# Layers 0 and 1 of a four-layer graph network: one-value-a-token rows spread through DRAM, attention applied to x before W, seven lanes for five

## Chip, cores, metric

One core of one Trainium2 chip. The metric is the device time of one execution in microseconds, median of several runs. In the profile's lines PE is TensorE, PEld its weight loads, DVE VectorE, ACT ScalarE, POOL GpSimd and SPq the queue of SyncE, which issues the DMA transfers; L550 is line 550 of that kernel; a record is one TensorE instruction in the trace. Ratios are the mean time of one kernel's fast runs over the mean of the other's fast runs in the same rounds, so they are not quite the ratios of the medians quoted beside them. Kernels of one batch of experiments ran on one chip beside the kernel before; kernels of different batches are compared by these ratios.

## The reference

x is 64 graphs x 256 nodes x 128 features, fp32; adj is one 256 x 256 matrix of zeros and ones. Four layers, each `x = layernorm(x + layer(x))`. Only the first two are changed:

```python
# layer 0
h = x @ others_weight
u1, u2 = h @ a1, h @ a2                      # one value a token
e = leaky(u1[:, idx1] + u2[:, idx2], 0.1)    # idx1, idx2: index pairs of a 256 x 256 grid
out = softmax(where(adj > 0, e, NEG_BIG), axis=1) @ h + x @ self_weight
# layer 1
h = x @ W
e = leaky((h @ a_src)[:, :, None] + (h @ a_dst)[:, None, :], 0.2)   # again one value a token
out = elu(softmax(where(adj + I == 0, -1e9, e), axis=-1) @ h)
# layer 2: five steps of a gated recurrent unit over adj;  layer 3: Chebyshev sums
```

Both attention layers need rows in which every partition holds one value for each token.

## The kernel before

The work is cut into 32 units of two graphs (512 tokens). A plan, computed in Python when the kernel is built, simulates the engines with one assumed duration for every instruction, takes the ready instruction of the oldest unit each time, and issues all instructions in that static order. Five units ("lanes") are in flight. On the chip each engine then runs its own list in order: an instruction that waits holds everything behind it on its engine.

```python
LATENCY = {"pe": 220, "dve": 150, "act": 150, "pool": 200, "sp": 3000}   # ns, from issue's end to use

def seen_at(self, t, by):            # when task `by` may count on task t
    return t.end if t.eng != by.eng else t.off + self.OWN[t.eng]
...
t.end = t.off + self.LATENCY[e] + t.wait

# layer 0, per unit (T = 512 tokens)                                       ... cut
xT = feature_major(u, L)                                    # 4 transposes
matmul(ps_c, wc_b, xT)                                      # L408: the row, by a broadcast matrix
matmul(ps_d[:, b:b+1], xb[:, b, k:N:2], wu[:, k:k+1])       # L412: x4, one column each
matmul(hx[b][:, c], xb[:, b, c*P:(c+1)*P], wx0)             # L423: x [W, self], 256 columns, x4
...                                                         # scores, exp, sums
matmul(hxv(b)[:, ic, 1], p[...], h[...])                    # L458: attention times h, x8
# layer 1
xT = feature_major(u, L)                                    # 4 transposes
matmul(ps_h[b][...], xb[:, b, c*P:(c+1)*P], wx1)            # L473: x4
matmul(ps_e, ws_b, xT)                                      # L477: the row
activation(e[:, g], ps_e[:, b*N:(b+1)*N], Prelu, bias=h[:, g, D:D+1])   # L486
...
matmul(ov()[:, ic], p[...], h[...])                         # L504: attention times h, x8
```

The softmax here doesn't subtract the row's maximum and nothing guards it: scores larger than these inputs give would overflow.

## Time and profile before

| | before |
|---|---|
| median, range | 1639.08 us, 1638.92 to 1639.25 (4 runs) |
| span, TensorE busy | 1637.2 us, 1615.9 us |
| mean granted TensorE clock | 0.999 |
| sum of TensorE's waits that the trace names | 13.7 us |

The prediction shows the engine shares, the chain and the waits. Two more lines of the page are needed for comparison: the granted clock in 40 slices (tenths of full speed), and the DMA packets by size.

```profile
PEclk9999999999999999999999999999999999999999
DMA packets 36731, 19.42 MB, mean 12 GB/s; under 512 B 2465, under 2 KB 36513, under 8 KB 36641
```

TensorE keeps 0.9 or more of its clock in every slice (0.999 on average), and 2465 of 36731 packets are under 512 bytes.

### The profile page before, as it was taken

The page shows a single profiled execution, that of the slowest core. Times are in us where ns is not written, and L with a number is a line of the kernel's source. Part 1 is how long each engine was busy: PE and PEld are TensorE (multiplying, and loading weights), DVE is VectorE, ACT ScalarE, POOL GpSimd, SP SyncE. Part 2 cuts the span into 40 slices and gives each one's busy share as a digit, 9 for nine tenths or more (in the row PEclk, how much of TensorE's full clock was granted, in tenths as well). Part 3 has the DMA queues.
Part 4 walks back from the last instruction along what each step waited for, and adds up shares of the span by engine and source line. Part 5 has one row for each costly group of instructions (what it writes and reads, how often), then busy time and mean ns, then how long its engine had stood idle before and what let it go on. Part 6 is the DMA issues. An engine that isn't in the chain of part 4 may idle for free.

```text
span 1637.2 us, 18751 instructions
## 1 busy us (share of the span) xinstructions
PE 1615.9 (99%) x6999; PEld 1095.2 (67%) x6999; DVE 950.4 (58%) x2214; ACT 820.2 (50%) x1602; POOL 145.7 (9%) x134
## 2 busy tenths in 40 slices
PE   8899999999999999999999999999999999999998
PEld 7556667666667666676666666667666667765566
DVE  6844556655556655466555665555656556763544
ACT  4644445544554545454455544545545544654542
POOL 0100001100001100011000110001101011100001
PEclk9999999999999999999999999999999999999999
DMA  9000000000000000000000000000000000000000
GB/s 241 1 0 7 7 7 8 7 1 7 7 7 7 7 1 7 7 8 7 1 7 7 7 7 1 7 7 7 7 1 7 7 7 7 7 1 0 1 7 26
DMA packets 36731, 19.42 MB, mean 12 GB/s; under 512 B 2465, under 2 KB 36513, under 8 KB 36641
## 3 DMA queue, kind: packets, MB, share of 16 engines
q1 hardware_dynamic: 36640, 18.23, 4.2%
q8 instruction: 55, 0.90, 0.2%
q14 instruction: 36, 0.29, 0.1%
HBM read 9.84 MB, written 8.39 MB: 11 GB/s over the span
## 4 chain that ended last, share of the span: by engine, by line
PE 94%; DVE 3%; ACT 1%; POOL 0%; issue 0%; DMA 0%; POOLq 0%; DVEq 0%; ACTq 0%
PE ps L543 41%; PE ps L527 20%; PE ps L597 7%; PE ps L570 4%; PE ps L604 3%; PE ps L423 3%; PE ps L375 3%; PE ps L504 3%; PE ps L458 3%; PE ps L408 2%; PE ps L473 2%; PE ps L477 2%; PE ps L412 1%; DVE x L395 1%; DVE st L386 0%; POOL rstd L391 0%
## 5 line engine op out<-in xcount | busy, mean ns | idle before, releaser
L543 PE MATMUL ps<-m,gT 128*128 128x512 f32 x960 | 463.7, 595 | 1.0 <-ACT e L549 0.6
L391 POOL TENSOR_TENSOR rstd<-ve,nhalf 128x4 f32<-128x4 f32 x128 | 145.0, 1134 | 1485.7 <-DVE ve L388 1459.0
L543 PEld LDWEIGHTS ps<-m,gT 128*128 128x128 f32 x960 | 173.1, 190 | 135.3 <-issue 116.2
L527 PE MATMUL ps<-adjT,ht 128*128 128x256 f32 x1024 | 253.6, 381 | 0.5 <-ACT ht L574 0.5
L551 DVE SCALAR_TENSOR_TENSOR e<-e,xT 128x512 f32<-128x512 f32 x160 | 110.3, 690 | 205.0 <-ACT e L549 204.5
L527 PEld LDWEIGHTS ps<-adjT,ht 128*128 128x128 f32 x1024 | 188.1, 190 | 54.9 <-issue 27.4
L562 DVE TENSOR_TENSOR p<-p,xT 128x512 f32<-128x512 f32 x160 | 110.3, 689 | 175.8 <-ACT p L556 175.3
L558 ACT ACTIVATE e<-ps,bias 128x512 f32<-128x512 f32 x160 | 109.9, 687 | 146.6 <-PE ps L543 146.6
L539 ACT COPY m<-ps 128x512 f32<-128x512 f32 x160 | 93.7, 585 | 174.4 <-PE ps L527 168.8
L543 PE MATMUL ps<-xT,gT 128*128 128x512 f32 x320 | 164.2, 595 | 0.5 <-ACT xT L377 0.5
L543 PE MATMUL ps<-e,u5T 128*128 128x512 f32 x320 | 163.0, 597 | 0.9 <-DVE e L551 0.8
L549 ACT ACTIVATE e<-ps,bias 128x512 f32<-128x512 f32 x160 | 109.9, 687 | 106.7 <-PE ps L543 106.0
L527 PE MATMUL ps<-adjT,x 128*128 128x256 f32 x512 | 143.6, 380 | 0.0
L570 PEld LDWEIGHTS ps<-ident,xT 128*128 128x128 f32 x640 | 83.7, 141 | 76.6 <-issue 53.4
L556 ACT ACTIVATE p<-ps,bias 128x512 f32<-128x512 f32 x160 | 109.9, 687 | 35.2 <-PE ps L543 34.8
L574 ACT COPY ht<-ps 128x512 f32<-128x512 f32 x128 | 74.6, 585 | 97.6 <-PE ps L570 96.8
L563 DVE SCALAR_TENSOR_TENSOR p<-e,p 128x512 f32<-128x512 f32 x160 | 110.2, 689 | 21.8 <-ACT e L558 18.7
L570 PE MATMUL ps<-ident,xT 128*128 128x128 f32 x640 | 118.7, 274 | 0.6 <-DVE xT L565 0.4
L395 DVE TENSOR_SCALAR x<-ps,st,rstd 128x128 f32<-128x128 f32 x256 | 93.4, 404 | 41.6 <-POOL rstd L391 41.0
L375 PE MATMUL ps<-ident,x 128*128 128x128 f32 x512 | 112.5, 276 | 1.6 <-DVE x L395 1.1
L377 ACT COPY xT<-ps 128x512 f32<-128x512 f32 x128 | 74.6, 585 | 78.6 <-PE ps L375 78.1
L565 DVE SCALAR_TENSOR_TENSOR xT<-p,xT 128x512 f32<-128x512 f32 x160 | 110.0, 687 | 2.9
(107 smaller groups left out, 2046.4 us busy)
## 6 DMA issues: line engine op xcount, KB each, us to landing
x<-in_x_dram SPq DMA_DIRECT2D x32, 256.0 KB, 5.5
out_dram<-x SPq DMA_DIRECT2D x32, 256.0 KB, 2.3
wk<-in_L_gnn_weight_dram SPq DMA_DIRECT2D x1, 448.0 KB, 5.2
gate<-in_L_gnn_w_w_dram SPq DMA_DIRECT2D x3, 128.0 KB, 3.4
adj_t<-in_adj_dram SPq DMA_DIRECT2D x1, 256.0 KB, 2.6
u<-in_L_gnn_u_w_dram SPq DMA_DIRECT2D x2, 64.0 KB, 3.0
wo<-L_gnn_others_weight_dram SPq DMA_DIRECT2D x1, 64.0 KB, 2.3
wself<-n_L_gnn_self_weight_dram SPq DMA_DIRECT2D x1, 64.0 KB, 2.8
```

Source lines behind the costliest of these rows:

```text
L375: add(PE, 110, lambda g=g: nc.tensor.transpose(ps.ap[:, g * P : (g + 1) * P], X[u].ap[:, g // NC, g % NC, :], ident.ap), (X[u], ident), (ps,))
L391: add(POOL, 1050, lambda: nc.gpsimd.tensor_tensor(rstd.ap, ve.ap, nhalf.ap, op=ALU.pow), (ve, nhalf), (rstd,))
L527: add(PE, mm_ns(N), lambda b=b, mc=mc: nc.tensor.matmul(ps.ap[:, b * N : (b + 1) * N], (src.ap if len(src.ap.shape) == 4 else src.ap.rearr ...
L543: add(PE, mm_ns(T), lambda: nc.tensor.matmul(ps.ap, w(), rhs.ap, start=start, stop=stop, skip_group_check=True), (c, rhs), (ps,))
L549: add(ACT, 600, lambda ps_g=ps_g: nc.scalar.activation(r.ap, ps_g.ap, AF.Tanh, bias=bias2.ap[:, 1:2], scale=0.5), (ps_g, bias2), (r,))
L551: add(DVE, 600, lambda h=h: nc.vector.scalar_tensor_tensor(r.ap, r.ap, 1.0, h.ap, op0=ALU.add, op1=ALU.mult), (r, h), (r,))
L556: add(ACT, 600, lambda ps_v=ps_v: nc.scalar.activation(v.ap, ps_v.ap, AF.Tanh, bias=bias2.ap[:, 2:3]), (ps_v, bias2), (v,))
L562: add(DVE, 600, lambda h=h: nc.vector.tensor_sub(v.ap, v.ap, h.ap), (v, h), (v,))
L563: add(DVE, 600, lambda: nc.vector.scalar_tensor_tensor(v.ap, z.ap, 1.0, v.ap, op0=ALU.add, op1=ALU.mult), (v, z), (v,))
L565: add(DVE, 600, lambda h=h, new=new: nc.vector.scalar_tensor_tensor(new.ap, v.ap, 0.5, h.ap, op0=ALU.mult, op1=ALU.add), (v, h), (new,))
L570: add(PE, 110, lambda g=g, h=h, ps_t=ps_t: nc.tensor.transpose(ps_t.ap[:, g * P : (g + 1) * P], h.ap[:, g * P : (g + 1) * P], ident.ap), ( ...
L597: add(PE, mm_ns(N), lambda k=k, src=src, c=c, b=b: nc.tensor.matmul(view(c)[:, :, b, :], bn(src.ap)[:, b, c * P : (c + 1) * P], w3.ap[:, k ...
```

## The change

Intent: take work off TensorE, which is the bound. Attention is applied to x (layer 1), which makes the result feature-major without transposes; rows and pair sums come from extra columns of other products, are stored to DRAM and loaded back with a partition broadcast. Two lanes more are to cover the longer way. The first three units (`DIRECT = 3`) make their rows with broadcast transposes on TensorE instead.

```diff
-LANES = 5
-LEAD = 20
+LANES = 7
+LEAD = 10
+DIRECT = 3
+        c["cu"] = cell(f"cu_{k}", [P, 3, G])
+        c["esd"] = cell(f"esd_{k}", [P, G, 2])
+    def to_row(row, src, view, n):
+        add("sp", 450, lambda: nc.sync.dma_start(row.ap[:, 0 : P * n].rearrange("o (p n) -> (o p) n", p=P), view()), (src,), (row,))
+    def from_row(t, row):
+        add("sp", 450, lambda: nc.sync.dma_start(t.ap, row.ap.rearrange("o n -> (o n)").partition_broadcast(P)), (row,), (t,),
+            wait=2500)
+    def on_all(u, t, row, src, view):
+        if u >= DIRECT:
+            to_row(row, src, view, G)
+            from_row(t, row)
+            return t, lambda: t.ap.rearrange("q (p b c) -> q b c p", b=UB, c=NC)
+        ...                                   # else: 4 transposes into PSUM
 layer 0:
+        row, rv = on_all(u, lc, L["row"], cu, lambda: cu.ap[:, 2])
+            to_row(L["rowu"], cu, lambda: cu.ap[:, 0:2].rearrange("p k g -> p (k g)"), 2 * G)
+            ...                               # two loads of u4 from rowu
+            add(DVE, 100, lambda: nc.vector.tensor_add(d.ap, u4.ap[:, 0:3:2], u4.ap[:, 12:15:2]), (u4,), (d,))
+            add(DVE, 120, ... tensor_mul(esd.ap[:, b * NC : (b + 1) * NC, :], yv()[:, :, D : D + 2], ...), (y, rstd), (esd,))
 layer 1:
-        xT = feature_major(u, L)
-        ...                                   # L473, L477 and the copies of h
+        es, ev = on_all(u, L["m"], L["row"], esd, lambda: esd.ap[:, :, 0])
-            add(ACT, 400, ... activation(e, ps_e, Prelu, bias=h.ap[:, g, D : D + 1]) ...)
+            add(ACT, 400, ... activation(e, ev()[:, b], Prelu, bias=esd.ap[:, g, 1:2]) ...)
+        ...                                   # x p: 8 records of 256 columns; then W
```

(x tiles become a ring of 14 and are loaded as lanes free up; the products of weights at the start are composed anew and centred. Both are cut here.)

More of the change, by code (lines that the diff above doesn't have):

```diff
@@ L190 @@
     PE, DVE, ACT, POOL = "pe", "dve", "act", "pool"
+    C0 = D + 5
     const = ctx.enter_context(tc.tile_pool(name="const", bufs=1))
     psum = ctx.enter_context(tc.tile_pool(name="psum", bufs=1, space=bass.MemoryType.PSUM))
+    dram = ctx.enter_context(tc.tile_pool(name="dram", bufs=1, space=bass.MemoryType.DRAM))
     def sb(name, shape):
@@ L217 @@
     out_u = out.rearrange("(u b) (c p) d -> u p b c d", b=UB, p=P)
-    X = {}
+    xs, X = [cell(f"x{k}", [P, UB, NC, D]) for k in range(2 * LANES)], {}
     def load_x(u):
-        X[u] = load(f"x{u}", x_u[u], [P, UB, NC, D], 1000)
-    adj_t = load("adj_t", adj.rearrange("(c p) j -> p c j", p=P), [P, NC, N])
+        X[u] = c = xs[u % len(xs)]
+        add("sp", 1000, lambda: nc.sync.dma_start(c.ap, x_u[u]), (), (c,))
+    w1 = load("w1", W, [D, D])
+    asd = cell("asd", [D, 2])
+    for k, a in enumerate((a_src, a_dst)):
+        add("sp", 450, lambda k=k, a=a: nc.sync.dma_start(asd.ap[:, k : k + 1], a), (), (asd,))
     wo = load("wo", others_weight, [D, D])
@@ L227 @@
     wself = load("wself", self_weight, [D, D])
+    adj_t = load("adj_t", adj.rearrange("(c p) j -> p c j", p=P), [P, NC, N])
     load_x(1)
-    w1 = load("w1", W, [D, D])
-    asd = cell("asd", [D, 2])
-    for k, a in enumerate((a_src, a_dst)):
-        add("sp", 450, lambda k=k, a=a: nc.sync.dma_start(asd.ap[:, k : k + 1], a), (), (asd,))
     load_x(2)
@@ L243 @@
     wk = load("wk", weight_1, [D, D, 7], 1500)
-    for u in range(4, NU):
+    for u in range(4, LANES):
         load_x(u)
@@ L290 @@
     add(DVE, 420, lambda: nc.vector.tensor_scalar(mask1.ap, mask1.ap, 0.0, None, op0=ALU.is_gt), (mask1,), (mask1,))
-    def projected(name, w, vecs):
-        wT = transposed(name + "T", [(w, w.ap)])
-        ps, t = bank(), cell(name, [P, 2])
-        add(PE, 150, lambda: nc.tensor.matmul(ps.ap[:, 0:2], wT.ap[:, 0], vecs.ap, start=True, stop=True),
-            (wT, vecs), (ps,))
-        add(DVE, 150, lambda: nc.vector.tensor_copy(t.ap, ps.ap[:, 0:2]), (ps,), (t,))
-        return t
-    wu = projected("wu", wo, att)
@@ L301 @@
-    wc = cell("wc", [P, 1])
-    add(DVE, 150, lambda: nc.vector.tensor_add(wc.ap, wu.ap[:, 0:1], wu.ap[:, 1:2]), (wu,), (wc,))
-    wc_b = cell("wc_b", [P, P])
-    add(DVE, 230, lambda: nc.vector.tensor_copy(wc_b.ap, wc.ap.to_broadcast([P, P])), (wc,), (wc_b,))
-    wx0 = cell("wx0", [P, 2, D])
-    add(DVE, 150, lambda: nc.vector.tensor_copy(wx0.ap[:, 0], wo.ap), (wo,), (wx0,))
-    add(DVE, 250, lambda: nc.vector.tensor_add(wx0.ap[:, 1], wself.ap, ident.ap), (wself, ident), (wx0,))
-    wsd = projected("wsd", w1, asd)
@@ L311 @@
-    ws_b = cell("ws_b", [P, P])
-    add(DVE, 230, lambda: nc.vector.tensor_copy(ws_b.ap, wsd.ap[:, 0:1].to_broadcast([P, P])), (wsd,), (ws_b,))
-    wx1 = cell("wx1", [P, D + 1])
-    add(DVE, 150, lambda: nc.vector.tensor_copy(wx1.ap[:, 0:D], w1.ap), (w1,), (wx1,))
-    add(DVE, 150, lambda: nc.vector.tensor_copy(wx1.ap[:, D : D + 1], wsd.ap[:, 1:2]), (wsd,), (wx1,))
+    centre = cell("centre", [P, P])
+    add(DVE, 150, lambda: nc.vector.tensor_scalar_add(centre.ap, ident.ap, -1.0 / D), (ident,), (centre,))
@@ new lines, in product @@
+    def product(ps, at, n, lhs, lhs_ap, rhs, rhs_ap):
+        add(PE, mm_ns(n), lambda: nc.tensor.matmul(ps.ap[:, at : at + n], lhs_ap(), rhs_ap(), start=True, stop=True,
+                                                   skip_group_check=True), (lhs, rhs), (ps,))
+    wx1 = cell("wx1", [P, D + 1])
+    w1cT = cell("w1cT", [P, D])
+    ps_w1, ps_w1T = bank(), bank()
+    product(ps_w1T, 0, D, w1, lambda: w1.ap, centre, lambda: centre.ap)
+    add(DVE, 230, lambda: nc.vector.tensor_copy(w1cT.ap, ps_w1T.ap[:, 0:D]), (ps_w1T,), (w1cT,))
@@ new lines @@
+    product(ps_w1, 0, D, centre, lambda: centre.ap, w1, lambda: w1.ap)
+    add(DVE, 230, lambda: nc.vector.tensor_copy(wx1.ap[:, 0:D], ps_w1.ap[:, 0:D]), (ps_w1,), (wx1,))
+    add(DVE, 60, lambda: nc.vector.memset(wx1.ap[:, D : D + 1], 1.0 / D), (), (wx1,))
+    right0 = cell("right0", [P, C0])
+    ps_r = bank()
+    add(DVE, 150, lambda: nc.vector.tensor_copy(right0.ap[:, 0:D], centre.ap), (centre,), (right0,))
+    product(ps_r, 0, 2, w1cT, lambda: w1cT.ap, asd, lambda: asd.ap)
+    add(DVE, 100, lambda: nc.vector.tensor_copy(right0.ap[:, D : D + 2], ps_r.ap[:, 0:2]), (ps_r,), (right0,))
@@ new lines @@
+    add(DVE, 100, lambda: nc.vector.tensor_copy(right0.ap[:, D + 2 : D + 4], att.ap), (att,), (right0,))
+    add(DVE, 100, lambda: nc.vector.tensor_add(right0.ap[:, D + 4 : D + 5], att.ap[:, 0:1], att.ap[:, 1:2]),
+        (att,), (right0,))
+    woT = transposed("woT", [(wo, wo.ap)])
+    add(DVE, 250, lambda: nc.vector.tensor_add(wself.ap, wself.ap, ident.ap), (wself, ident), (wself,))
+    wselfT = transposed("wselfT", [(wself, wself.ap)])
+    wx0, ws0 = cell("wx0", [P, C0]), cell("ws0", [P, D + 2])
@@ L318 @@
+    for t, wT, n in ((wx0, woT, C0), (ws0, wselfT, D + 2)):
+        ps = bank()
+        product(ps, 0, n, wT, lambda wT=wT: wT.ap[:, 0], right0, lambda n=n: right0.ap[:, 0:n])
+        add(DVE, 230, lambda t=t, n=n, ps=ps: nc.vector.tensor_copy(t.ap, ps.ap[:, 0:n]), (ps,), (t,))
     gs = [cell(f"gs{k}", [D, D]) for k in range(3)]
@@ L354, in lane_cells @@
             c[name] = Cell(c[at].ap.rearrange("p g n -> p (g n)")[:, half * T : (half + 1) * T])
-        c["h0"] = cell(f"h0_{k}", [P, G, D])
-        c["h1"] = cell(f"h1_{k}", [P, G, D + 2])
+        c["h0"] = cell(f"h0_{k}", [P, G, C0])
         c |= {name: cell(f"{name}_{k}", [P, G]) for name in ("nm", "s", "rs", "rstd", "ve")}
@@ L359, in lane_cells @@
         c["st"] = cell(f"st_{k}", [P, UB, 6])
-        add(DVE, 60, lambda: nc.vector.memset(c["h1"].ap[:, :, D + 1 : D + 2], 1.0), (), (c["h1"],))
+        c["u"] = cell(f"u_{k}", [P, 15])
+        c["cu"] = cell(f"cu_{k}", [P, 3, G])
+        c["esd"] = cell(f"esd_{k}", [P, G, 2])
+        for name, n in (("row", T), ("rowu", 2 * T + 2)):
+            c[name] = Cell(dram.tile([1, n], F32, tag=f"{name}_{k}", name=f"{name}_{k}"))
         return c
@@ L378, in feature_major, with layernorm @@
         return L[name]
-    def layernorm(u, L, pairs, swap=False):
+    def to_row(row, src, view, n):
[8 more added lines that the diff above has]
+            return t, lambda: t.ap.rearrange("q (p b c) -> q b c p", b=UB, c=NC)
+        ps = bank()
+        for g in range(G):
+            add(PE, 110, lambda g=g: nc.tensor.transpose(
+                ps.ap[:, g * P : (g + 1) * P], view()[:, g : g + 1].to_broadcast([P, P]), ident.ap), (src, ident), (ps,))
+        return ps, lambda: ps.ap.rearrange("q (b c p) -> q b c p", b=UB, c=NC)
+    def layernorm(u, L, pairs, swap=False, centred=False):
         st, ve, rstd = L["st"], L["ve"], L["rstd"]
@@ L394, in layernorm @@
                 b, ch = (j, k) if swap else (k, j)
+                if centred:
+                    add(DVE, 260, lambda k=k, j=j, b=b, ch=ch, view=view: nc.vector.tensor_scalar(
+                        X[u].ap[:, b, ch, :], view()[:, j, :], rstd.ap[:, 2 * k + j : 2 * k + j + 1], 1.0,
+                        op0=ALU.mult, op1=ALU.add), (c, rstd), (X[u],))
+                    continue
                 add(DVE, 260, lambda k=k, j=j, b=b, ch=ch, view=view: nc.vector.tensor_scalar(
@@ L406, in layer0 @@
         xb = bn(xT.ap)
-        ps_c, ps_d = bank(), bank()
-        tail = [add(PE, mm_ns(T), lambda: nc.tensor.matmul(ps_c.ap, wc_b.ap, xT.ap, start=True, stop=True),
-                    (xT, wc_b), (ps_c,))]
+        lc, d, e, p, h, u4, cu = L["m"], L["d"], L["e"], L["p"], L["h0"], L["u"], L["cu"]
+        nm, s, rs = L["nm"], L["s"], L["rs"]
         for b in range(UB):
-            for k in range(2):
-                tail.append(add(PE, 240, lambda b=b, k=k: nc.tensor.matmul(
-                    ps_d.ap[:, b : b + 1], xb[:, b, k : N : 2], wu.ap[:, k : k + 1], start=(k == 0), stop=(k == 1)),
-                    (xT, wu), (ps_d,)))
@@ L416, in layer0 @@
-        hx = [bank() for _ in range(UB)]
-        def hxv(b):
-            return hx[b].ap.rearrange("p (c k d) -> p c k d", c=NC, k=2)
-        for b in range(UB):
-            for c in range(NC):
-                add(PE, mm_ns(N), lambda b=b, c=c: nc.tensor.matmul(
-                    hx[b].ap[:, c * N : (c + 1) * N], xb[:, b, c * P : (c + 1) * P],
-                    wx0.ap.rearrange("p k d -> p (k d)"), start=(c == 0), stop=True, skip_group_check=True),
-                    (xT, wx0), (hx[b],), tail)
@@ L427, in layer0 @@
-        lc, d, nd, e, p = L["m"], L["d"], L["nd"], L["e"], L["p"]
-        nm, s, rs, h = L["nm"], L["s"], L["rs"], L["h0"]
-        add(ACT, 600, lambda: nc.scalar.activation(lc.ap, ps_c.ap, AF.Prelu, alpha=0.1), (ps_c,), (lc,))
-        add(ACT, 160, lambda: nc.scalar.activation(d.ap, ps_d.ap[:, 0:UB], AF.Prelu, alpha=0.1), (ps_d,), (d,))
-        ev = e.ap.rearrange("p (b c) n -> p b c n", b=UB)
-        add(DVE, 600, lambda: nc.vector.tensor_add(
-            ev[:, :, :, 0:P], lc.ap.rearrange("p (b i c) -> p b c i", b=UB, c=NC),
-            neg0.ap[:, :, 0:P].rearrange("p (o c) n -> p o c n", o=1).to_broadcast([P, UB, NC, P])), (lc, neg0), (e,))
+            hx = bank()
@@ new lines, in hv @@
+            def hv(hx=hx):
+                return hx.ap[:, 0 : NC * C0].rearrange("p (c k) -> p c k", c=NC)
+            for c in range(NC):
+                add(PE, mm_ns(C0), lambda b=b, c=c, hv=hv: nc.tensor.matmul(
+                    hv()[:, c, :], xb[:, b, c * P : (c + 1) * P], wx0.ap, start=(c == 0), stop=True,
+                    skip_group_check=True), (xT, wx0), (hx,))
+            add(ACT, 400, lambda b=b, hv=hv: nc.scalar.copy(h.ap[:, b * NC : (b + 1) * NC, :], hv()), (hx,), (h,))
@@ new lines, in layer0 @@
+        add(DVE, 120, lambda: nc.vector.tensor_copy(cu.ap, h.ap[:, :, D + 2 : D + 5].rearrange("p g k -> p k g")), (h,), (cu,))
+        add(DVE, 100, lambda: nc.vector.scalar_tensor_tensor(
+            cu.ap[:, 2], cu.ap[:, 2], 0.1, cu.ap[:, 2], op0=ALU.mult, op1=ALU.max), (cu,), (cu,))
+        row, rv = on_all(u, lc, L["row"], cu, lambda: cu.ap[:, 2])
+        if u >= DIRECT:
+            to_row(L["rowu"], cu, lambda: cu.ap[:, 0:2].rearrange("p k g -> p (k g)"), 2 * G)
+            for c in range(NC):
+                add("sp", 450, lambda c=c: nc.sync.dma_start(
+                    u4.ap[c * P // 2 : (c + 1) * P // 2],
+                    L["rowu"].ap[:, c : c + 2 * T].rearrange("o (i n) -> (o i) n", n=16)[:, 0:15]), (L["rowu"],), (u4,))
+            add(DVE, 100, lambda: nc.vector.tensor_add(d.ap, u4.ap[:, 0:3:2], u4.ap[:, 12:15:2]), (u4,), (d,))
+            ds = d
+        else:
+            ds = bank()
+            for b in range(UB):
+                for k in range(2):
+                    add(PE, 240, lambda b=b, k=k: nc.tensor.matmul(
+                        ds.ap[:, b : b + 1], xb[:, b, k : N : 2], wx0.ap[:, D + 2 + k : D + 3 + k],
+                        start=(k == 0), stop=(k == 1)), (xT, wx0), (ds,))
@@ L435, in layer0 @@
+        add(ACT, 160, lambda: nc.scalar.activation(d.ap, ds.ap[:, 0:UB], AF.Prelu, alpha=0.1), (ds,), (d,))
+        ev = e.ap.rearrange("p (b c) n -> p b c n", b=UB)
+        for b in range(UB):
+            add(DVE, 330, lambda b=b: nc.vector.tensor_add(
+                ev[:, b, :, 0:P].rearrange("p k (c i) -> p k c i", c=NC), rv()[:, b].rearrange("p c (i k) -> p k c i", k=2),
+                neg0.ap[:, :, 0:P].rearrange("p k (c i) -> p k c i", c=NC)), (row, neg0), (e,))
         for b in range(UB):
@@ L445, in layer0 @@
         for g in range(G):
-            add(ACT, 620, lambda g=g: nc.scalar.activation(
+            add(ACT, 400, lambda g=g: nc.scalar.activation(
                 p.ap[:, g, :], e.ap[:, g, :], AF.Exp, bias=nm.ap[:, g : g + 1], accum_out=s.ap[:, g : g + 1]),
                 (e, nm), (p, s))
-        add(DVE, 120, lambda: nc.vector.reciprocal(rs.ap, s.ap), (s,), (rs,))
-        for b in range(UB):
-            add(DVE, 350, lambda b=b: nc.vector.tensor_mul(
-                h.ap[:, b * NC : (b + 1) * NC, :], hxv(b)[:, :, 0, :],
-                rs.ap[:, b * NC : (b + 1) * NC].rearrange("p (c o) -> p c o", o=1).to_broadcast([P, NC, D])),
-                (hx[b], rs), (h,))
@@ L455, in layer0, with yv @@
-        for b in range(UB):
+        tail = [add(DVE, 120, lambda: nc.vector.reciprocal(rs.ap, s.ap), (s,), (rs,))]
+        add(DVE, 700, lambda: nc.vector.tensor_mul(
+            h.ap[:, :, 0 : D + 2], h.ap[:, :, 0 : D + 2],
+            rs.ap.rearrange("p (g o) -> p g o", o=1).to_broadcast([P, G, D + 2])), (h, rs), (h,))
+        esd, rstd = L["esd"], L["rstd"]
+        ys = []
+        for b in range(UB):
+            y = bank()
+            def yv(y=y):
+                return y.ap[:, 0 : NC * (D + 2)].rearrange("p (c k) -> p c k", c=NC)
+            ys.append((y, yv))
+            for c in range(NC):
+                add(PE, mm_ns(D + 2), lambda b=b, c=c, yv=yv: nc.tensor.matmul(
+                    yv()[:, c, :], xb[:, b, c * P : (c + 1) * P], ws0.ap, start=(c == 0), stop=False,
+                    skip_group_check=True), (xT, ws0), (y,), tail)
@@ L456, in layer0 @@
             for ic in range(NC):
                 for kc in range(NC):
-                    add(PE, mm_ns(P), lambda b=b, ic=ic, kc=kc: nc.tensor.matmul(
-                        hxv(b)[:, ic, 1, :], p.ap[:, b * NC + kc, ic * P : (ic + 1) * P], h.ap[:, b * NC + kc, :],
-                        start=False, stop=True, skip_group_check=True), (p, h), (hx[b],))
-        layernorm(u, L, [(hx[b], lambda b=b: hxv(b)[:, :, 1, :]) for b in range(UB)])
-    def layer1(u, L):
-        xT = feature_major(u, L)
-        xb = bn(xT.ap)
-        H = D + 2
-        ps_h = [bank() for _ in range(UB)]
-        tail = []
-        for b in range(UB):
-            for c in range(NC):
-                tail.append(add(PE, mm_ns(D + 1), lambda b=b, c=c: nc.tensor.matmul(
-                    ps_h[b].ap[:, c * H : c * H + D + 1], xb[:, b, c * P : (c + 1) * P], wx1.ap,
-                    start=(c == 0), stop=True, skip_group_check=True), (xT, wx1), (ps_h[b],)))
-        ps_e = bank()
-        add(PE, mm_ns(T), lambda: nc.tensor.matmul(ps_e.ap, ws_b.ap, xT.ap, start=True, stop=True),
-            (xT, ws_b), (ps_e,), tail)
-        h, e, p = L["h1"], L["e"], L["p"]
-        for b in range(UB):
-            add(ACT, 300, lambda b=b: nc.scalar.copy(
-                h.ap[:, b * NC : (b + 1) * NC, 0 : D + 1],
-                ps_h[b].ap[:, 0 : NC * H].rearrange("p (c k) -> p c k", c=NC)[:, :, 0 : D + 1]), (ps_h[b],), (h,))
@@ new lines, in layer0 @@
+                    add(PE, mm_ns(D + 2), lambda b=b, ic=ic, kc=kc, yv=yv: nc.tensor.matmul(
+                        yv()[:, ic, :], p.ap[:, b * NC + kc, ic * P : (ic + 1) * P], h.ap[:, b * NC + kc, 0 : D + 2],
+                        start=False, stop=(kc == NC - 1), skip_group_check=True), (p, h), (y,))
+        layernorm(u, L, [(y, lambda yv=yv: yv()[:, :, 0:D]) for y, yv in ys], centred=True)
+        for b, (y, yv) in enumerate(ys):
+            add(DVE, 120, lambda b=b, yv=yv: nc.vector.tensor_mul(
+                esd.ap[:, b * NC : (b + 1) * NC, :], yv()[:, :, D : D + 2],
+                rstd.ap[:, b * NC : (b + 1) * NC].rearrange("p (c o) -> p c o", o=1).to_broadcast([P, NC, 2])),
+                (y, rstd), (esd,))
@@ L484, in layer1 @@
+    def layer1(u, L):
+        H = D + 1
+        esd, e, p = L["esd"], L["e"], L["p"]
+        es, ev = on_all(u, L["m"], L["row"], esd, lambda: esd.ap[:, :, 0])
         for g in range(G):
@@ L486, in layer1 @@
             add(ACT, 400, lambda g=g, b=b: nc.scalar.activation(
-                e.ap[:, g, :], ps_e.ap[:, b * N : (b + 1) * N], AF.Prelu, bias=h.ap[:, g, D : D + 1], alpha=0.2),
-                (ps_e, h), (e,))
+                e.ap[:, g, :].rearrange("p (c n) -> p c n", c=NC), ev()[:, b], AF.Prelu, bias=esd.ap[:, g, 1:2], alpha=0.2), (es, esd), (e,))
         ef, pf = e.ap.rearrange("p g n -> p (g n)"), p.ap.rearrange("p g n -> p (g n)")
@@ L493, in layer1 @@
             mask1.ap.rearrange("p (o c) n -> p o (c n)", o=1).to_broadcast([P, UB, NC * N])), (e, mask1), (p,))
+        ps_x, px = bank(), L["xT0"]
+        for b in range(UB):
+            for jc in range(NC):
+                add(PE, mm_ns(N), lambda b=b, jc=jc: nc.tensor.matmul(
+                    ps_x.ap[:, b * N : (b + 1) * N], X[u].ap[:, b, jc, :], p.ap[:, b * NC + jc, :],
+                    start=(b == 0 and jc == 0), stop=(jc == NC - 1), skip_group_check=True), (X[u], p), (ps_x,))
+        add(ACT, 500, lambda: nc.scalar.copy(px.ap, ps_x.ap), (ps_x,), (px,))
         rs, hp, hn, th = L["rs"], L["ht"], L["m"], L["xT1"]
-        ex = Cell(L["h0"].ap.rearrange("p g d -> p (g d)"))
+        ex = L["h0"]
+        exf = ex.ap.rearrange("p g d -> p (g d)")[:, 0:T]
         for b in range(UB):
@@ L502, in layer1 @@
             for ic in range(NC):
-                for jc in range(NC):
-                    add(PE, mm_ns(H), lambda b=b, ic=ic, jc=jc, ov=ov: nc.tensor.matmul(
-                        ov()[:, ic, :], p.ap[:, b * NC + jc, ic * P : (ic + 1) * P], h.ap[:, b * NC + jc, :],
-                        start=(ic == 0 and jc == 0), stop=True, skip_group_check=True), (p, h), (ps_o,))
+                add(PE, mm_ns(H), lambda b=b, ic=ic, ov=ov: nc.tensor.matmul(
+                    ov()[:, ic, :], bn(px.ap)[:, b, ic * P : (ic + 1) * P], wx1.ap,
+                    start=(ic == 0), stop=True, skip_group_check=True), (px, wx1), (ps_o,))
             r = rs.ap[:, b * NC : (b + 1) * NC].rearrange("p (c o) -> p c o", o=1)
-            add(DVE, 120, lambda r=r, ov=ov: nc.vector.reciprocal(r, ov()[:, :, D + 1 : D + 2]), (ps_o,), (rs,))
+            add(DVE, 120, lambda r=r, ov=ov: nc.vector.reciprocal(r, ov()[:, :, D : D + 1]), (ps_o,), (rs,))
             add(DVE, 350, lambda b=b, r=r, ov=ov: nc.vector.tensor_mul(
@@ L513, in layer1 @@
         add(ACT, 550, lambda: nc.scalar.activation(th.ap, hn.ap, AF.Tanh, scale=0.5), (hn,), (th,))
-        add(ACT, 550, lambda: nc.scalar.activation(ex.ap, hn.ap, AF.Exp), (hn,), (ex,))
+        add(ACT, 550, lambda: nc.scalar.activation(exf, hn.ap, AF.Exp), (hn,), (ex,))
         xf = X[u].ap.rearrange("p b c d -> p (b c d)")
@@ L517, in layer1 @@
             (hp, X[u]), (hp,))
-        add(DVE, 600, lambda: nc.vector.scalar_tensor_tensor(th.ap, ex.ap, 1.0, th.ap, op0=ALU.add, op1=ALU.mult),
+        add(DVE, 600, lambda: nc.vector.scalar_tensor_tensor(th.ap, exf, 1.0, th.ap, op0=ALU.add, op1=ALU.mult),
             (ex, th), (th,))
@@ L610, in spawn @@
     def spawn(u, lane):
+        if u + LANES < NU:
+            load_x(u + LANES)
         for layer in (layer0, layer1, layer2, layer3):
```

## The prediction

> **What bounds the kernel now.** I read the page first (engine shares, slices, chain), then the groups, then the waits of TensorE, then its timeline at mid-run and at the start. From the page:
>
> ```profile
> PE 1615.9 (99%) x6999; PEld 1095.2 (67%) x6999; DVE 950.4 (58%) x2214; ACT 820.2 (50%) x1602; POOL 145.7 (9%) x134
> PE   8899999999999999999999999999999999999998
> PE 94%; DVE 3%; ACT 1%; POOL 0%; issue 0%; DMA 0%; POOLq 0%; DVEq 0%; ACTq 0%
> ```
>
> TensorE is busy nearly all the time and makes 94% of the chain that ended last. A busy PE could still be one that waits inside its pipeline, so I looked at its waits and its spacing. Its two largest waits of the run are
>
> ```profile
> PE ps L273 <- DMA adj_t<-in_adj_dram: 3.5, 1, 3.5
> PE ps L504 <- DVE p L491: 3.2, 3, 1.2
> ```
>
> which is nothing against 1637 us. The timeline at mid-run (start, duration, group, count) gives the true price of a record: the distance to the next start, divided by the count.
>
> ```profile
> 630.85 1.89 PE L527 MATMUL ps<-adjT,ht 128*128 128x256 f32 x8
> 632.58 5.31 PE L543 MATMUL ps<-m,gT 128*128 128x512 f32 x12
> 637.73 1.88 PE L543 MATMUL ps<-e,u5T 128*128 128x512 f32 x4
> 639.44 1.95 PE L504 MATMUL ps<-h,p 128*128 128x130 f32 x16
> 641.23 1.02 PE L408 MATMUL ps<-xT,wc_b 128*128 128x512 f32 x2
> ...
> 646.33 0.49 PE L570 MATMUL ps<-ident,xT 128*128 128x128 f32 x3
> 646.66 0.76 PE L412 MATMUL ps<-wu,xT 128*128 128x1 f32 x6
> 647.28 1.96 PE L543 MATMUL ps<-m,gT 128*128 128x512 f32 x4
> ```
>
> A 512-column record takes (637.73 - 632.58)/12 = 0.429 us, 256 columns (632.58 - 630.85)/8 = 0.216, 130 columns (641.23 - 639.44)/16 = 0.112, a transpose (646.66 - 646.33)/3 = 0.11, and a record of one column still (647.28 - 646.66)/6 = 0.103. The groups count two records for each fp32 matmul of the source (960 for 480 products at L543) and one for a transpose. Counts of the groups times these prices add up to about 1595 us. The other 42 us of the span are lost; by the same sum over windows, 17 of them in the first 80 us, 8 at the end, the rest thinly in between. So time follows PE work, and the change must be counted in PE records.
>
> **What the Trainium skill says.** "TensorE: Matmul & The Clock Gate", section Back-to-back issue gap, gives the isolated gap of a warm matmul as N/2.4 + 2.5 ns. For one fp32 record this trace shows twice the column term, 512/1.2 + 2.5 = 429 ns and 256/1.2 + 2.5 = 216 ns: it agrees in form, at two array passes a record. "FP8 and Floating Point Precision", section TensorE Precision Notes, says that true fp32 takes four passes; two records of two passes each agree with it. The first page, section LDWEIGHTS, prices a weight load as its columns over 1.2, so 107 ns for 128; the one-column records at 0.103 to 0.107 us agree: they are paid as weight loads. "DMA: Bandwidth & Descriptors", section Anatomy of one DMA, puts the fixed cost at about 2 us, mostly the wait for the write receipt; that is its GpSimd path. Here the 256 KB output stores, issued by SyncE, land after 2.3 us (median), which fits.
>
> **The change, part by part, PE time per pair of batches ("unit", 32 of them).** I use 0.429, 0.216, 0.111 (128 to 130 columns), 0.105 (one column) and 0.109 (transpose).
>
> Layer 0 before: 4 transposes 0.44; the row broadcast by matmul (L408) 2 x 0.429 = 0.86; the one-column products (L412) 8 x 0.105 = 0.84; x times [W, self] (L423) 8 x 0.216 = 1.73; attention times h (L458) 16 x 0.111 = 1.78. Sum 5.64. After: 4 transposes 0.44; x times a 133-column matrix 8 x 0.114 = 0.91 (133/1.2 + 2.5); x times self 8 x 0.111 = 0.89; attention 1.78. Sum 4.01. The row and the pair sums come out of the extra columns and travel through DRAM.
>
> Layer 1 before: transposes 0.44; x W (L473) 8 x 0.111 = 0.89; broadcast (L477) 0.86; attention (L504) 1.78. Sum 3.96. After: attention times x as 8 records of 256 columns 1.73; then W, 0.89. Sum 2.62. No transposes of x, because the x-stationary form makes the result feature-major at once; e_src and e_dst are made in layer 0.
>
> Saved: 9.60 - 6.63 = 2.97 us a unit. The first three units keep the direct way (4 + 4 transposes and the 8 one-column records, 1.71 us more), so they save 1.26 each. Total 29 x 2.97 + 3 x 1.26 = 90 us. Layers 2 and 3, 40 us a unit, are untouched.
>
> The other engines: VectorE loses L432 (0.68) and the two L451 (0.84 from PSUM) and gains two half-sized adds with a stride (estimate 0.82), the 520-column scaling (0.70, as L520's 0.688), and small ones (about 0.8): +0.8 on 29.7 us a unit. ScalarE loses about 0.6. With a unit at 47 us of PE, VectorE stands at 65%, ScalarE at 53%: neither becomes the bound on average. DMA adds 7 small or 256 KB transfers a unit against a DMA mean of 12 GB/s: no load, only latency.
>
> **What eats some of it: the start.** While no unit is in layer 2, VectorE sets the pace: layers 0 and 1 need some 14 us of it for under 10 (now 6.6) us of PE. Before, the first unit reached layer 2 at 66 us, and layer 1 was held to 45 us by the second half of the attention vector, whose load came last in SyncE's queue:
>
> ```profile
> L232 SPq DMA_DIRECT2D asd<-in_L_gnn_a_dst_dram x1: 832/832/832, 34.5 to 34.5; - x1
> ```
>
> Afterwards that load stands behind some 20 issues instead of 50 (about 0.5 us each, with 3 MB at 241 GB/s ahead of it), so I estimate 15 us to landing. But now the very first matrix of layer 0 needs it (through the composed right-hand side), so layer 0 starts at about 18 us instead of 11, with only transposes to do before. Chain of the first unit by durations above: layer 0 about 14 us, layer 1 about 16, and 8 for others' VectorE and ScalarE work in between: layer 2 at 55 to 60 us. Until then PE gets about 28 us of work, so 30 to 32 us are lost against 17 before: +12 to +15 us. Part of the PE saving falls just where PE was not the bound. The end (last layer 3, normalization, store) is unchanged at 7 to 8 us.
>
> Sum: 1639 - 90 + 13 = 1562; I shade it to **1558 us**, because seven lanes give PE more ready work while it fills, -4.9%.
>
> **Rivals.** (a) *The wait moves to DMA latency.* Each row now takes a store, a wait for it, and a broadcast load: two landings of 2.3 to 3 us, twice a unit, in one in-order SyncE queue, and VectorE and ScalarE are in order behind it. If the landings come later than the planner assumes (3.45 us for one, 5.95 for the broadcast), an in-order VectorE stalls and older units behind it with it. A stall of 1 us in each of 58 row trips that reaches PE makes +58, so about 1615. For it: the static order, the four-hop chain. Against it: the planner's allowances are above the 2.3 us landing seen; young units have the lowest priority, so their results are usually early; L608 shows SyncE idle almost all the time. (b) *The start costs nothing:* the planner interleaves well, full 90 us and fewer pipeline losses: 1545. (c) *VectorE becomes the bound in the mix of layers 0 and 1:* strided reads slow, two lanes in these layers at once. The largest plausible strided penalty (a doubling of two adds and four activations) is about 3 us a unit on engines with 16 us of slack: no effect but at the start, 1570. (d) *PE waits on weight loads*, as records become narrower: all new ones are at least 128 columns, above the 107 ns of a load; no effect.
>
> **Range and chances.** Between (b) and a third of (a) plus a bad start: 1538 to 1592. Within 2% needs over 1606, that is half of the gain lost to rival (a): 0.09. Slower by over 2%: 0.01. Faster by over 2%: 0.90.
>
> **What would show it.** PE still at 97% or more, with L408, L412, L477, and half of the x transposes gone but for three units; one group of 256-column attention records x256, one of 133 columns x256, each at 0.216 and 0.113 us spacing; from about 80 us to the end no PE wait over 1 us. The first layer-2 record at 55 to 60 us and 25 to 35 us lost in the first 80. The rows' landings at 2 to 3.5 us. Wrong, if PE shows regular idle time before layer 0 or 1 work ended by a DMA or by VectorE that itself waited for one, or if PE work fell by clearly less than 90 us.

## The result, and the profile after

**1773.21 us** median (1770.81 to 1774.61, 4 runs), ratio 1.0817 (95% interval 1.0798 to 1.0836): 8% slower, where -4.9% was predicted. Correct output.

| | before | after |
|---|---|---|
| span | 1637.2 us | 1772.8 us |
| TensorE busy, records | 1615.9 us, 6999 | 1591.3 us, 6541 |
| sum of TensorE's named waits | 13.7 us | 173.6 us |
| mean granted clock | 0.999 | 0.953 |

From the page of the kernel after: engine shares, slices, granted clock, packets, and the chain that ended last by engine and by line.

```profile
PE 1591.3 (90%) x6541; PEld 1065.5 (60%) x6541; DVE 960.5 (54%) x2368; ACT 827.3 (47%) x1570; POOL 140.2 (8%) x134
PE   7799979986989879989997899888988778999998
PEclk9999989998999989999999999999999889999999
DMA packets 73386, 35.06 MB, mean 20 GB/s; under 512 B 31696, under 2 KB 65744, under 8 KB 73296
PE 57%; DMA 22%; DVE 12%; ACT 6%; SPq 2%; issue 1%; POOL 1%; POOLq 0%; DVEq 0%; ACTq 0%
PE ps L614 28%; PE ps L598 13%; DMA row<-esd 11%; DMA m<-row 5%; PE ps L668 4%; PE ps L641 3%; PE ps L675 3%; ACT e L550 2%; DMA rowu<-cu 2%; PE ps L561 2%; DMA u<-rowu 2%; DVE st L430 1%; PE ps L531 1%; DVE x L444 1%; DMA row<-cu 1%
```

No other engine became busy: VectorE and ScalarE have a smaller share than before. TensorE has holes through the whole run, and the chain that was 94% TensorE is now 22% DMA, half of it one transfer, `row<-esd`. The DMA issues show what is special about it (operation, count, KB each, median us from issue to landing):

```profile
m<-row SPq DMA_DIRECT2D x58, 256.0 KB, 3.8
u<-rowu SPq DMA_DIRECT2D x58, 3.8 KB, 3.0
row<-cu SPq DMA_DIRECT2D x29, 2.0 KB, 2.2
row<-esd SPq DMA_DIRECT2D x29, 2.0 KB, 7.0
```

Two stores of the same 2 KB, to the same kind of row: the one from `cu` (layer 0) lands after 2.2 us, the one from `esd` (layer 1) after 7.0. `cu[:, 2]` is four neighbouring values in each partition, one 16-byte run. `esd[:, :, 0]` is every second value of `[P, G, 2]`, four runs of 4 bytes. The waits (us in total, times, longest) show whom it holds:

```profile
ACT e L550 <- DMA m<-row: 133.0, 26, 9.8
DVE d L483 <- DMA u<-rowu: 70.5, 22, 15.8
```

and, in the queue of SyncE, the broadcast load that waits for the store:

```profile
SPq L408 <- DMA row<-esd: 203.9, 29, 10.7
```

One such case in the timeline (start, duration, engine, group; in brackets the idle time just before and its end):

```profile
585.70 0.56 SPq L404 DMA_DIRECT2D row<-esd  x1
...
592.92 1.89 PE L668 MATMUL ps<-w,m 128*128 128x256 f32 x8
593.97 0.33 SPq L408 DMA_DIRECT2D m<-row  x1
...
597.45 2.64 ACT L550 ACTIVATE e<-m,esd 128x256 f32<-128x256 f32 x4 [5.92 <-DMA m<-row]
600.12 1.06 ACT L553 ACTIVATE e<-e 128x1024 f32<-128x1024 f32 x1
601.09 0.63 ACT L672 COPY e<-ps 128x256 f32<-128x256 f32 x2
601.21 1.22 DVE L554 TENSOR_TENSOR p<-e,mask 128x1024 f32<-128x1024 f32 x1 [9.86 <-ACT e L553]
601.49 3.66 PE L675 MATMUL ps<-e,a2T 128*128 128x256 f32 x8 [5.16 <-ACT e L672]
```

The store is issued at 585.7, the load can only follow at 594.0, and the row is there at 597.4: 11.7 us. The plan allowed 0.45 + 0.45 + 3 + 2.5 = 6.4: store and load are both tasks of SyncE, so `seen_at` lets the load follow as soon as the store is issued, not when it has landed. So the plan had put L550 of a *young* unit ahead of L672, a copy for an *older* unit in layer 3, whose input had long been there. ScalarE, in order, waits 5.9 us for the row, then runs L550 and L553, and only then the copy; TensorE waits 5.2 us for that copy.

And TensorE comes back slow: eight records of 256 columns in 3.66 us, against 1.89 for the eight of 592.92. The windows view gives the granted clock of the two stretches (start and end, length; busy us and count of PE, PEld, DVE, ACT, POOL; PEclk; DMA share; GB/s):

```profile
596.40:601.40 5.00, 0.00 (x0) 0.00 (x0) 0.19 (x1) 3.92 (x7) 0.00 (x0) 1.00 0.04 10
601.50:604.90 3.40, 3.40 (x8) 2.75 (x9) 1.66 (x3) 0.70 (x2) 0.00 (x0) 0.50 0.00 0
```

After the idle stretch it runs at half clock for 3.4 us. The Trainium skill has this ("TensorE: Matmul & The Clock Gate", Part 1: the clock falls to 4/8 after at least one idle window of about 3.4 us, and comes back after a busy one); this trace agrees, with 0.50 after 5.2 us of idling. This stall so costs about 7 us: 5.2 of idling and 3.66 - 1.89 = 1.8 of slower records. In the whole trace the clock stands at half in 29 stretches of 3.4 to 13.7 us, 170 us together.

### The profile page after: what moved, and what is told of

Its sections match the earlier page's. It is cut to its first block, busy times and chain, and to the rows that moved or that the text cites. A ratio compares the mean times of both kernels' runs of the same rounds, so it can differ in the third digit from the quotient of the medians.

```text
span 1772.8 us, 18253 instructions
## 1 busy us (share of the span) xinstructions
PE 1591.3 (90%) x6541; PEld 1065.5 (60%) x6541; DVE 960.5 (54%) x2368; ACT 827.3 (47%) x1570; POOL 140.2 (8%) x134
## 2 busy tenths in 40 slices
DMA packets 73386, 35.06 MB, mean 20 GB/s; under 512 B 31696, under 2 KB 65744, under 8 KB 73296
## 4 chain that ended last, share of the span: by engine, by line
PE 57%; DMA 22%; DVE 12%; ACT 6%; SPq 2%; issue 1%; POOL 1%; POOLq 0%; DVEq 0%; ACTq 0%
PE ps L614 28%; PE ps L598 13%; DMA row<-esd 11%; DMA m<-row 5%; PE ps L668 4%; PE ps L641 3%; PE ps L675 3%; ACT e L550 2%; DMA rowu<-cu 2%; PE ps L561 2%; DMA u<-rowu 2%; DVE st L430 1%; PE ps L531 1%; DVE x L444 1%; DMA row<-cu 1%
## 5 line engine op out<-in xcount | busy, mean ns | idle before, releaser
L614 PE MATMUL ps<-m,gT 128*128 128x512 f32 x960 | 477.7, 608 | 44.2 <-ACT m L610 25.0
L598 PE MATMUL ps<-adjT,ht 128*128 128x256 f32 x1024 | 271.0, 397 | 38.6 <-ACT ht L645 38.4
L435 POOL TENSOR_TENSOR rstd<-ve,nhalf 128x4 f32<-128x4 f32 x128 | 139.5, 1092 | 1626.8 <-DVE ve L432 1498.2
L598 PEld LDWEIGHTS ps<-adjT,ht 128*128 128x128 f32 x1024 | 195.8, 199 | 108.6 <-ACT ht L645 47.6
L614 PE MATMUL ps<-e,u5T 128*128 128x512 f32 x320 | 168.6, 614 | 4.2 <-DVE e L622 4.2
L614 PE MATMUL ps<-xT,gT 128*128 128x512 f32 x320 | 168.4, 609 | 3.0 <-ACT xT L399 3.0
L550 ACT ACTIVATE e<-m,esd 128x256 f32<-128x256 f32 x116 | 81.2, 743 | 133.0 <-DMA m<-row 133.0
L641 PE MATMUL ps<-ident,xT 128*128 128x128 f32 x640 | 128.5, 277 | 9.0 <-DVE xT L636 8.9
L598 PEld LDWEIGHTS ps<-adjT,x 128*128 128x128 f32 x512 | 82.8, 193 | 31.7 <-issue 17.7
L430 DVE BATCH_NORM_STATS2 st<-ps 128x6 f32<-128x256 f32 x128 | 54.3, 426 | 83.1 <-PE ps L675 69.3
```

The source lines that it names most:

```text
L435: add(POOL, 1050, lambda: nc.gpsimd.tensor_tensor(rstd.ap, ve.ap, nhalf.ap, op=ALU.pow), (ve, nhalf), (rstd,))
L550: add(ACT, 400, lambda g=g, b=b: nc.scalar.activation(e.ap[:, g, :].rearrange("p (c n) -> p c n", c=NC), ev()[:, b], AF.Prelu, bias=esd.ap ...
L598: add(PE, mm_ns(N), lambda b=b, mc=mc: nc.tensor.matmul(ps.ap[:, b * N : (b + 1) * N], (src.ap if len(src.ap.shape) == 4 else src.ap.rearr ...
L614: add(PE, mm_ns(T), lambda: nc.tensor.matmul(ps.ap, w(), rhs.ap, start=start, stop=stop, skip_group_check=True), (c, rhs), (ps,))
L641: add(PE, 110, lambda g=g, h=h, ps_t=ps_t: nc.tensor.transpose(ps_t.ap[:, g * P : (g + 1) * P], h.ap[:, g * P : (g + 1) * P], ident.ap), ( ...
```

## Experiments

In each experiment the quoted text is what was expected before the run.

**Theory A:** the 4-byte store is late. **Theory P:** late *against the plan* is what counts: not the length of the trip, but that the in-order engines were scheduled for a shorter one. **Rivals:** B, any trip through DRAM costs this; or seven lanes; or the new small operations and reordered products themselves.

### e1: 16-byte runs in layer 1's store

```diff
-        c["esd"] = cell(f"esd_{k}", [P, G, 2])
+        c["esd"] = cell(f"esd_{k}", [P, 2, G])
-        es, ev = on_all(..., lambda: esd.ap[:, :, 0])
+        es, ev = on_all(..., lambda: esd.ap[:, 0])
```

> One change to the changed kernel: esd is laid out [P, 2, G] instead of [P, G, 2], so that the layer-1 store of e_src reads 16-byte runs as the layer-0 store does. Theory A (the layer-1 store is cut into 512 pieces of 4 bytes, lands after 7.0 us instead of the 2.2 us of the layer-0 store, and the activation that waits for the row holds the in-order ScalarE): about 11,000 packets fewer (384 x 29), the store lands at 2.0 to 2.6 us, the wait of the layer-1 activation for the broadcast falls from 133 us to under 30, time 1600 to 1670. Theory B (any trip through DRAM costs about this, whatever its runs): store quicker but time still above 1720.

1607.04 us (ratio 0.981, 0.9795 to 0.9825), 166 us less. No planned time is altered, and TensorE's list of instructions came out identical to that of the kernel after (6541 of 6541), so this is the store alone. Packets, issues and waits of e1:

```profile
DMA packets 62250, 35.06 MB, mean 22 GB/s; under 512 B 20560, under 2 KB 54608, under 8 KB 62160
row<-esd SPq DMA_DIRECT2D x29, 2.0 KB, 1.6
```
```profile
DVE d L483 <- DMA u<-rowu: 55.9, 25, 8.5
ACT e L550 <- DMA m<-row: 3.5, 4, 1.2
```

73386 - 62250 = 11136 = 384 x 29 packets fewer: 512 packets a store have become 128. It lands after 1.6 us instead of 7.0 (sooner than the 2.0 to 2.6 foretold), and ScalarE's wait falls from 133 us to 3.5. A holds, B falls. But 1607 is not 1558: VectorE still waits for the pair sums (`u<-rowu`), whose two hops the plan also books too short, and TensorE's named waits are still 55 us.

### e2: the slow store kept, the plan corrected

```diff
-        return t.end if t.eng != by.eng else t.off + self.OWN[t.eng]
+        return t.end if t.eng != by.eng or t.eng == "sp" else t.off + self.OWN[t.eng]
     # plan only: store of esd wait=4500, broadcast load wait=1000 (was 2500)
```

> The changed kernel with its 4-byte store, only the static plan's allowances altered: a DMA that needs another DMA is planned after that one's landing, the layer-1 store is allowed 7.95 us and the broadcast 4.45 us. Theory P (it is not the length of the trip that costs but that it is longer than the plan allowed, so that in-order engines are made to wait while other ready work is queued behind): PE waits nearly vanish although the store still lands at 7 us; 1555 to 1600 us. Theory A in its plain form (length costs): still above 1700. If seven lanes cannot cover the longer trip, between.

1599.69 us (ratio 0.9761, 0.9746 to 0.9775), at the upper edge of what P foretold. The store is as slow as ever:

```profile
row<-esd SPq DMA_DIRECT2D x29, 2.0 KB, 7.4
```
```profile
DVE e L495 <- DMA m<-row: 19.8, 9, 4.4
ACT e L550 <- DMA m<-row: 14.1, 6, 7.5
DVE d L483 <- DMA u<-rowu: 6.5, 2, 3.5
```

With no transfer made faster, 173 us are gone. So the 7 us by themselves are not what costs most, but that the plan did not book them: A says why the row is late, P how lateness becomes time. One sign of P missed: TensorE's named waits fall from 173.6 to 49.6 us, they do not nearly vanish. The edit alters the rule and two allowances at once, and what each is worth was not separated.

### e3: no trips at all

```diff
-DIRECT = 3
+DIRECT = 32
```

> The changed kernel with DIRECT = 32: no unit uses DRAM, all make their rows by broadcast transposes on TensorE; seven lanes and the reordered products stay. PE work rises by 29 x 1.71 = 50 us over the changed kernel's 1505, to about 1555; if the trips are the whole loss, the lost time falls from 268 us to about 40 to 55 and the time is 1595 to 1612, faster than the kernel before. If seven lanes, the reordered products or the new small operations of layer 0 and 1 are at fault, it stays above 1650.

1593.49 us (ratio 0.9723, 0.9707 to 0.9739), just under the expected range. Its page:

```profile
PE 1574.0 (99%) x7005; PEld 1085.4 (68%) x7005; DVE 948.2 (60%) x2339; ACT 799.2 (50%) x1570; POOL 138.5 (9%) x134
```

TensorE is full again. So seven lanes, the reordered products and nearly all the new small operations do no harm; the loss of the changed kernel lies in the trips and what goes with them (the strided reads of the rows and the adds of the loaded pair sums are gone here too).

### e4: five lanes

```diff
-LANES = 7
-LEAD = 10
+LANES = 5
+LEAD = 20
```

> The changed kernel with five lanes and LEAD 20 as before. If seven lanes are what hurts, under 1700; if the trips are the cause, 1750 to 1850, the same waits for the row on ScalarE.

1817.97 us (ratio 1.1093): worse still, with ScalarE waiting 137.0 us for the row. Seven lanes are not the culprit.

### e5, e6, e7, e8: how much the plan allows

All four have the 16-byte layout of e1 and e2's rule that a DMA which needs another is planned after that one's landing. They differ only in what the plan assumes, in us from issue to use; e6 to e8 also book what the strided readers of the row take (660 instead of 400 ns for L550, 560 instead of 330 for L495):

| | store | broadcast | pair sums | strided readers | median us | ratio (95%) |
|---|---|---|---|---|---|---|
| e8_short | 1.95 | 1.45 | 1.45 | booked | 1628.20 | 0.9931 (0.9917 to 0.9946) |
| e5_both | 3.45 | 4.95 | 3.95 | no | 1567.79 | 0.9561 (0.9545 to 0.9576) |
| e6_durs | 3.45 | 4.95 | 3.95 | booked | 1560.85 | 0.9522 (0.9508 to 0.9536) |
| e7_slack | 5.45 | 7.45 | 6.45 | booked | 1555.26 | 0.9489 (0.9475 to 0.9503) |

> The 16-byte layout of e1 together with the planning of e2, its allowances set to what e1 measured: store 3.45 us, broadcast 4.95 us, pair-sum loads 3.95 us. If lateness against the plan is the cause, the causes of e1 and e2 partly overlap and the remainder shrinks: PE waits under 20 us in all, time 1545 to 1580, faster than e1, e2 and the direct form. If something else limits the form with DRAM trips (strided reads of the row, SyncE's order), it stays at 1590 to 1600.

> As e5, and the plan is told what the strided readers of the row take: 660 ns (not 400) for the layer-1 activation, 560 ns (not 330) for the layer-0 add. In the trace the first takes 743 to 759 ns in place of 485 from PSUM, the second 611 in place of 415. If the plan's errors of this kind are part of the remainder, 10 to 30 us less than e5; if only the DMA allowances matter, within 5 us of e5.

> As e6 with 2 to 2.5 us more allowance on each of the three kinds of transfer than measured. If lateness is all that costs, and seven lanes have room for longer trips, this is as fast as e6 or faster (1540 to 1570), although every trip is planned longer. If the length of the trip costs, it is 10 us or more slower than e6.

> As e6 with allowances 1.5 to 3.5 us shorter than measured (store 1.95, broadcast 1.45, pair sums 1.45 us): the transfers themselves are the same as in e5 to e7. Theory P foretells that ScalarE and VectorE wait again on the rows: 29 units x 2 rows x 2 to 3 us, most of it reaching PE, 1640 to 1720. If planned time is not the cause, as e6.

The transfers are the same in all four (the broadcast lands after 3.9 to 4.0 us). Booked too short, both readers of the rows wait again (e8):

```profile
ACT e L550 <- DMA m<-row: 59.7, 26, 5.1
DVE e L495 <- DMA m<-row: 59.4, 26, 5.7
```

at +67 us over e6. P foretold the waits (119 us of them), but 1640 to 1720 us: only about half of the waiting reached the time. e5 fell in its range, with 28.3 us of TensorE's waits instead of under 20; e6 came 7 us under e5, between its two forecasts; e7 fell in its range. Booked with room (e7), the trace names no wait of ScalarE or VectorE for a row, and the page reads as the kernel before did:

```profile
PE 1524.4 (98%) x6541; PEld 1036.1 (67%) x6541; DVE 963.1 (62%) x2368; ACT 826.2 (53%) x1570; POOL 145.2 (9%) x134
PE   8899999999999999999999999999999999999998
PEclk9999999999999999999999999999999999999999
PE 94%; DVE 3%; ACT 1%; DMA 1%; SPq 0%; issue 0%; POOL 0%; POOLq 0%; DVEq 0%; ACTq 0%
```

**e7 is the fastest version by its median, 5.1% under the kernel before** (e9's interval overlaps with its). It has the same 6541 TensorE records as the kernel after; they take 1524.4 us instead of 1591.3. The 220 us between their spans are these 67 (some 58 of them are half clock: half of TensorE's busy time inside the half-clock stretches) and 153 of idle TensorE (1772.8 - 1591.3 = 181.5 against 28.4).

### e9 to e12: what is left

e9: the second half of layer 1's attention vector is no longer chained behind the first (two cells for one). e10: e9 with 2 to 3 us more allowance. e11: e7 with `LANES = 5`, `LEAD = 20` (`LEAD` weighs the order of the last units only). e12: e7 with the old 4-byte layout, its allowance 2 us above its landing.

> As e7, and the second half of layer 1's attention vector is no longer chained behind the first in the plan, so its load is issued early. In the kernel after it was issued at 11.6 us and the first layer-0 matrix ran at 18.4 us. Expected: layer 0 starts by 13 us, layer 2 of the first unit 4 to 6 us earlier than in e7, time 3 to 6 us under e7: 1549 to 1552. If VectorE sets the pace of the start anyway, within 2 us of e7.

> As e9 with a further 2 to 3 us of allowance on each transfer (store 7.45, broadcast 10.45, pair sums 8.45 us). The same time as e9 within 4 us if trip length is free at seven lanes; clearly slower (over 8 us) if the lanes run out of cover.

> As e7 with five lanes and LEAD 20. With the plan right, five lanes hold 5 x 47 = 235 us of PE work per unit in flight, above the chain of one unit; I expect 1555 to 1575. If seven lanes are needed to cover the planned trips, over 1585.

> The layer-1 store left at 4-byte runs (7 us and more to landing), everything else as e7, its allowance 2 us above that landing. Theory P in its strong form: the runs' size does not matter once it is planned for, 1553 to 1565, as e7. If the slow store costs by itself[...], 15 us or more above e7.

| | median us | ratio (95%) |
|---|---|---|
| e9_start | 1558.64 | 0.9511 (0.9495 to 0.9526) |
| e10_slack2 | 1567.12 | 0.9561 (0.9547 to 0.9575) |
| e11_lanes5 | 1597.57 | 0.9749 (0.9731 to 0.9767) |
| e12_4byte_slack | 1572.28 | 0.9593 (0.9578 to 0.9607) |

- e9 missed: layer 0 starts at 8.7 instead of 19.1 us and the first unit's layer 2 at 51.2 instead of 56.1, but the end comes no sooner than in e7. By the windows view TensorE idles 11.0 us of the first 100, against 13.6 in e7, and then 10.8 us up to 1530, against 8.2: the gain is given back in small pieces in the middle. Why, I did not find.
- e10: 8.5 us (0.5%) over e9, on the side foretold if the lanes run out of cover.
- e11 missed: 1597.57, not 1555 to 1575. ScalarE and VectorE have no named wait for a row in it, TensorE's largest is 15.3 us. Once the trips are booked in full, seven lanes are 42 us faster than five; that five have too little other work to fill the trips is the likely reason, not a measured one.
- e12: with the plan right, the 4-byte runs cost about 1% more than 16-byte ones (17 us over e7), not the 10% of the kernel after against e1. By the measure set before the run P in its strong form fell, though most of the 17 us lie within what another order can make (below). Its slowest broadcast load landed after 12.2 us, against 5.2 in e7, and ScalarE still waited 7.6 us for rows.

Every variant that alters a planned time gets another static order throughout. e5, e6, e7, e9 and e10, all booked at or above the median landings, lie between 1555 and 1568 us; a difference of that size (0.8%) between such variants can be the order itself, and I do not assign it. That goes for e6 against e5, e10 against e9 and most of e12's 1%. The 67 us of e8 and the 173 of e2 are far above it, and e1 is free of it.

## Why the prediction was wrong

1. **TensorE's work** was predicted to fall by 90 us. It did: 1615.9 to 1524.4, 91.5 us, once the clock stays up (e7). This step was right, and e7's 1555 us lies at the predicted 1558 (its idle TensorE grew by 7 us, where 13 less a shading of 4 were expected).
2. **The start**: layer 0 at about 18 us (18.4 measured), first layer-2 record at 55 to 60 (57.8). Both were right, though e9 shows that the start matters less than argued.
3. **Other engines**: neither became the bound. The row's strided readers are slower (743 ns against 485 and 611 against 415), within the doubling allowed for; booking them in the plan went with 0.4% (e5 to e6), too little to assign. ScalarE did not lose the 0.6 us a unit that was forecast: its busy time rose from 820.2 to 827.3 us; VectorE's rose by 10.1 us, 0.3 a unit where 0.8 was forecast.
4. **The step that failed is the dismissal of rival (a)**: "the planner's allowances are above the 2.3 us landing seen". That landing belongs to a 256 KB store of long runs. It was carried over to a 2 KB store without looking at the runs that the store reads. The layout `[P, G, 2]` with the view `[:, :, 0]` stood in the diff. The Trainium skill warns of it ("DMA: Bandwidth & Descriptors", section Rules for kernel authors: a strided last dimension lowers to one descriptor per element); this trace agrees, with 512 packets a store and 7.0 us. The allowance was misread too: the prediction set 3.45 us for the store and 5.95 for the broadcast against the two landings, 9.4 together, but the plan never waited for the store's landing and allowed 6.4 for both. The chain of store, load issue and load took 11.7 us in the case shown. The pair sums were booked by the same rule, which is why the quick store alone (e1) stays at 1607 us; with the plan corrected as well (e5) it is 1568.
5. **Rival (a) was also mis-sized.** Its 58 us assumed 1 us lost in each of 58 trips, at full clock. Against the kernel before, 160 us more of idle TensorE (181.5 against 21.3) and 67 us of slower records, most of them at half clock, stand against the 91.5 saved: +160 + 67 - 91.5 = +135.5, the measured 1772.8 - 1637.2 = 135.6. "Young units have the lowest priority, so their results are usually early" is where the mechanism was misread: priority decides the place in the list when the plan is made; on the chip a late instruction of a young unit stands in front of an old one's.

Shown by experiment: the store's runs alone make 166 us (e1); a corrected plan makes 173 us without any faster transfer (e2); the two overlap, and both with room make 218 us (e7); no harm comes from lanes or products (e3, e4). The 28 us left between e7's span and its TensorE busy time are, by the windows view, 13.6 in the first 100 us, 6.6 in the last 23 and 8.2 between (before: 9.7, 7.1 in the last 22, and 4.5). Not settled: why e9's earlier start is given back, and how much of e2's gain is the rule and how much the allowances.

## What to carry to other kernels

When the instruction order is fixed before the run, a new kind of transfer needs its own measured latency in the plan, and a chain of transfers needs the sum of its landings; 2 us to spare did no harm here (e7 beside e6). A late row holds the in-order engine that waits for it, and so the ready work of other units behind it; in the case shown a TensorE that idled 5.2 us then ran at half clock for 3.4. Before crediting a DMA with the latency of another, count its contiguous runs on both sides; `[:, :, 0]` of a small array made one packet an element here. And when a change slows a kernel although the work on the bound fell as computed, repair the schedule before rejecting the change: here it turned +8.2% into -5.1%.

## What the Trainium skill lacked or had wrong

- "DMA: Bandwidth & Descriptors" says that a strided last dimension costs a descriptor per element, but gives no latency for it on SyncE's queue. Here 2 KB from 128 partitions to DRAM took 1.4 to 2.5 us (medians of the runs) as 128 runs of 16 bytes and 7.0 to 7.4 us as 512 runs of 4 bytes.
- "TensorE: Matmul & The Clock Gate" gives its gaps for bf16 and no gap for fp32. Here an fp32 matmul is two records, each spaced 0.429 us at 512 columns and 0.216 at 256; a one-column record still takes 0.103 us.
- "SBUF — State Buffer" names 16-byte lines and a penalty for each new line, without a size. Here a 256-column activation took 743 ns from SBUF at a stride of 16 bytes, against 485 from PSUM without one; the VectorE add of 256 columns took 611 from SBUF at a stride of 32 bytes, against 415 from PSUM at 8. The memory differs as well as the stride, so the stride's own share is not separated.
- No page says how the lateness of one DMA passes on through an in-order engine to other work under a static order. Here 5.3 us of lateness against the plan went with a 5.2 us hole on TensorE (kernel after, at 597 us); only the 3.4 us at half clock that followed are on the page cited above.
